# Turning a row of attention weights: by way of DRAM, or straight from place to place on chip

## The chip, the cores and the metric

The kernel runs on one core of one Trainium2 chip. A core has five engines that work side by side and wait for each other by semaphores: TensorE (PE, with its weight loads as PEld), VectorE (DVE), ScalarE (ACT), GpSimd (POOL) and SyncE (SP). Here SP does almost nothing but issue transfers; sixteen DMA engines carry them out. The metric is the time of one launch on the device in microseconds (us), median of several runs; less is better.

## The reference, cut to what matters

Two layers work on a graph of 3327 nodes with 256 features. Layer 0 makes two steps. In each, a full matrix and a sparse attention matrix are multiplied with the features:

```
A = _top_p_attention(Xa, W1, W2, W3)   # softmax(q k^T), smallest entries dropped, 0.9 of the mass kept
Xf = R @ Xf                            # R = (adj + I), rows normed
Xa = A @ Xa
Z = Z + Xf @ U1[n].T + Xa @ U2[n].T
```

Layer 1 is a graph attention over the neighbours in adj with 4 heads. All is float32.

The change touches A @ Xa. TensorE sums over partitions, so a tile of A has to lie with its columns (the nodes summed over) on the partitions. The softmax and the search for the cut need it the other way: rows on the partitions. So each block of A must be turned on the way.

## The kernel before, in words

**Tiles.** The 3327 nodes are padded to 26 tiles of 128. One "row" is a tile of 128 nodes of A, an array `e` of 128 partitions by 3328 floats (13,312 bytes per partition). There are 26 rows in each of the two steps, 52 in all. Every row goes through the same stages:

1. `logits` and `exps`: TensorE makes 128 x 3327 logits, ScalarE their exponentials into `e`.
2. `count`, `step`, `window`, `sort`, `choose`: ScalarE, GpSimd and VectorE find the cut.
3. `drop`: VectorE sets what is under the cut to zero, in three parts (columns 0 to 1023, 1024 to 2047, the rest).
4. The turn. VectorE's transpose turns 32 x 32 blocks in place, each within its own 32 partitions (`turn_blocks`, L1082). After that every block is right inside but stands in the wrong group of 32 partitions. In the kernel before, `put_blocks` (L1086) writes a part of the row to an array `blocks` in DRAM, and four `get_blocks` (L1091) read it back, one for each group of 32 partitions, each with 256-byte pieces. Per row that is three puts and twelve gets.
5. `attend_blocks` (L1098): 26 matrix products, one for each tile of columns, into one PSUM accumulator `acca`; then `attended` (L1102) scales the sum.
6. `finish1` or `finish2`: projections for the next step, or the layer norm for layer 1.

Beside it runs R @ Xf: `Full` loads each row tile of adj, turned already by the host, in seven transfers of four column tiles into four buffers `at` (L1117) and multiplies (L1123) into `accf`. These products don't wait for a row of A, so they fill TensorE while rows are being searched.

After both steps comes layer 1 (`attend_neighbours`): masks from adj (L1678, L1688, L1689), exponents on VectorE (L1700), products on TensorE (L1716, L1730).

**Order.** No engine chooses at run time. `Plan` takes every piece of work with an engine, a length, a rank, what it needs, which buffers it takes and gives, and a lag until others see its result, runs through time with these charges, and writes out one fixed order for each engine. On the chip each engine then follows its list and stops at the first piece whose data isn't there. For SP this means that a transfer at the head of the list holds back all transfers behind it, such as loads of `at`. The charges that matter here: a put 0.5 us with a lag of 8.0, a get 0.6 with 5.5, a load of `at` 0.4 with 4.0.

**Semaphores of transfers.** The transfers use eight semaphores in turn; one that takes up a semaphore waits for the transfer eight places before it.

**Buffers.** Five arrays hold rows `e` (four from `epool`, the fifth, `qq`, from `wpool`); a row keeps its array from its logits to its last attend. Small things are held in pools: `et` (three of 2 KB per partition, used for the statistics' copies, the masks of layer 1 and some loads), `f` (three), `at` (four).

Of the kernel before, what the change touches and what calls it, by code (L numbers as in the profile page):

```python
# [10 lines left out]
F32 = mybir.dt.float32  # L11
BF16 = mybir.dt.bfloat16
# [3 lines left out]
ALU = mybir.AluOpType  # L16
AX = mybir.AxisListType
PSUM = bass.MemoryType.PSUM

P = 128  # L20
N = 3327
NT = 26
NP = NT * P
D = 256
DA = 64
# [21 lines left out]
PIECES = 16  # L47
PART = 1024
PIECE_AT = [PART * (k // 5) + 205 * (k % 5) for k in range(PIECES)] + [N]
QUANTILE = (6.4004942, -10.1694914, 9.3637353, -4.4723851)  # L50

REACH = 40.0

BUFS = dict(kk=2, e=4, sc=6, f=3, xa=2, xt=2, kq=3, ystage=2, base=1, mv=4, cum=2)

# [531 lines left out]
def fast(  # L587
# [58 lines left out]
    with ExitStack() as l0:  # L646
        wpool = l0.enter_context(tc.tile_pool(name="wpool", bufs=1))
        small = l0.enter_context(tc.tile_pool(name="small", bufs=2))
        epool = l0.enter_context(tc.tile_pool(name="epool", bufs=4))
        scr = l0.enter_context(tc.tile_pool(name="scr", bufs=1))  # L650
        apool = l0.enter_context(tc.tile_pool(name="apool", bufs=4))
        etpool = l0.enter_context(tc.tile_pool(name="etpool", bufs=3))
        ps_l = l0.enter_context(tc.tile_pool(name="ps_l", bufs=2, space=PSUM))
# [8 lines left out]

        kt = wpool.tile([P, 3 * 512 + P], F32, name="kt")
        kks = [wpool.tile([P, P + 2], F32, name=f"kk{k}") for k in range(2)]
        for kk in kks:
# [3 lines left out]
        rsum = wpool.tile([P, NT], F32, name="rsum")  # L669
        blocks = spill.tile([NT // 2, P, 2 * P], F32, name="blocks")  # L670

        gks = [wpool.tile([P, 2 * DA + 1], F32, name=f"gk{n}") for n in range(STEPS)]
        for gk in gks:
            GP.memset(gk, 0.0)
            GP.tensor_copy(gk[:DA, DA + 1 :], ident[:DA, :DA])

        stat = wpool.tile([P, 2, NT], F32, name="stat")
        sig, zadd, cn, cs = (wpool.tile([P, NT], F32, name=n) for n in ("sig", "zadd", "cn", "cs"))
# [19 lines left out]
        def weights():  # L698
            held = {}
            w1 = etpool.tile([P, 4, P], F32, name="et")  # L700
            w1 = w1[:, 0, :].rearrange("p (c o) -> p c o", c=2)
# [48 lines left out]
        def layer1_loads():  # L750

            late = wpool.tile([P, 2 * D + 2 * (H * FH + 2 * H)], F32, name="late")
            g_all, b_all = late[:, :D], late[:, D : 2 * D]
            wa = late[:, 2 * D :].rearrange("p (c o) -> p c o", c=2)
            a_all = etpool.tile([P, H, 2 * FH], F32, name="et")
            nc.sync.dma_start(g_all, ln_g.partition_broadcast(P))
            nc.sync.dma_start(b_all, ln_b.partition_broadcast(P))
            nc.sync.dma_start(a_all, gat_a.partition_broadcast(P))
            nc.sync.dma_start(wa[:, :, : H * FH], gat_w.rearrange("(c p) o -> p c o", p=P))
            return g_all, b_all, wa, a_all  # L760

        def layer1_scores(wa, a_all):

            prod = etpool.tile([P, 2, H, FH], F32, name="et")
            for k in range(2):
                for a in range(2):
                    V.tensor_mul(
                        prod[:, 0],
                        wa[:, k, : H * FH].rearrange("p (h f) -> p h f", h=H),
                        a_all[:, :, a * FH : (a + 1) * FH],  # L770
                    )
                    lo = H * FH + a * H
                    V.tensor_reduce(wa[:, k, lo : lo + H], prod[:, 0], AX.X, ALU.add)

# [34 lines left out]
        def stats(n, lo, hi, rank, needs, scaled):  # L809
# [13 lines left out]
            def copy(held, m):  # L823
                qg = etpool.tile([P, 4, P], F32, name="et").rearrange("p a b -> p (a b)")
                held["qg"] = qg[:, : 3 * (2 * DA + 1)].rearrange("p (a b) -> p a b", a=3)
                S.copy(held["qg"][:, :m, :], held["ps"][:, :m, :])
# [10 lines left out]
            for t0 in range(lo, hi, 2):  # L837
                held, m = {}, min(2, hi - t0)
                a = plan.put("PE", 0.25 * m, rank, product, held, t0, m, needs=[needs, scaled], take=["px"])
                a = plan.put("ACT", 0.45, rank, copy, held, m, needs=[a], take=["et"], give=["px"])  # L840
                ends.append(plan.put("DVE", 0.35 * m + 0.2, rank, square, held, t0, m, needs=[a], give=["et"]))

# [21 lines left out]

        plan = Plan(dict(rows=1, mvs=3, pl=2, px=2, acca=1, accf=1, et=3, at=4, y=1, e2=2, ec=1, mask=2, e5=1, qg=2, **BUFS))
        own_e = [[("e", "e5")[i % 5 == 2 - n] for i in range(NT)] for n in range(STEPS)]
# [3 lines left out]
        class Row:  # L870
# [7 lines left out]
            def __init__(self, n, i):  # L878
                self.n, self.i, self.pl, self.pt, self.et = n, i, {}, {}, {}

# [195 lines left out]

            def part(self, g):
                return self.e[:, g * PART : (g + 1) * PART if g < 2 else NP]

            def turn_blocks(self, g):  # L1080
                part = self.part(g).rearrange("p (g s t) -> p g t s", s=P, t=2)
                V.transpose(part, part)  # L1082

            def put_blocks(self, g):
                src = self.part(g).rearrange("p (g w) -> p g w", w=2 * P)
                nc.sync.dma_start(blocks[4 * g : 4 * g + src.shape[1]].rearrange("g p w -> p g w"), src)  # L1086

            def get_blocks(self, g, o):
                to = self.part(g)[o * P // 4 : (o + 1) * P // 4].rearrange("p (c w) -> p c w", w=P // 2)
                src = blocks[4 * g : 4 * g + to.shape[1] // 4, :, o * P // 2 : (o + 1) * P // 2]  # L1090
                nc.sync.dma_start(to, src.rearrange("g (b s) w -> s (g b) w", b=4))  # L1091

            def attend_blocks(self, js):
                for j in js:
                    if j == 0:
                        self.acc = ps_a.tile([P, D], F32, name="acca")
                    lhs = self.e[:, j // 2 * 256 : (j // 2 + 1) * 256].rearrange("p (q t) -> p t q", t=2)[:, j % 2, :]
                    T.matmul(self.acc, lhs, rhs[self.n][:, j, :], start=(j == 0), stop=(j == NT - 1))  # L1098
# [419 lines left out]
        def attention(row, rank, total, drops, right):  # L1518
            a = None
            come = []  # L1520
            for g in range(3):
                b = plan.put(
                    "DVE", 1.17 if g < 2 else 1.44, rank - 1.001, row.turn_blocks, g, needs=[drops[g]]
                )
                b = plan.put("SP", 0.5, rank - 1.0, row.put_blocks, g, needs=[b], lag=8.0)
                b = plan.put("", 0.0, -90.0, lambda: None, needs=[b], lag=0.0)
                come.append(
                    [plan.put("SP", 0.6, rank - 1.0, row.get_blocks, g, o, needs=[b], lag=5.5) for o in range(4)]
                )
            for j in range(0, NT - 2, 4):  # L1530
                js = range(j, j + 4 if j < 20 else NT)
                a = plan.put(
                    "PE", 0.432 * len(js), rank, row.attend_blocks, js, needs=[come[j // 8], a, right],
                    take=["acca"] * (j == 0), give=[own_e[row.n][row.i]] * (j == 20),
                )
            return plan.put("ACT", 0.4, rank - 2.7, row.attended, needs=[a, total], take=["xa"], give=["acca", "sc"])
# [26 lines left out]
        def attend_neighbours(rows, ends, done, fulls):  # L1563
# [80 lines left out]
            for b in range(4):  # L1644
# [14 lines left out]
                for j in range(NT):  # L1659
# [21 lines left out]

                    def mask(held=held, off=off):
                        m = etpool.tile([P, 4, P], F32, name="et").rearrange("p a b -> p (a b)").bitcast(BF16)
                        m = held["mask"] = m[:, :W]
                        A, B = (held.pop(g).rearrange("p i q -> p (i q)") for g in range(2))
                        A, B = A[:, off:], B[:, : W + off - 4 * P]
                        for to, src in ((m[:, : 4 * P - off], A), (m[:, 4 * P - off :], B)):
                            S.activation(src, src, AF.Relu)  # L1688
                            S.activation(to, src, AF.Sign)  # L1689
# [48 lines left out]

                    own = ["et", "mask"]
                    if b == 0 and j < 2:  # L1740
                        loads, own = plan.put("SP", 0.2, rank, load_first, needs=[opened[0]], lag=4.0), []
                        m_ = plan.put("ACT", 1.8, rank, mask_first, needs=[loads])
                    else:
# [197 lines left out]
        for n in range(STEPS):  # L1941
# [30 lines left out]
            if n == 0:  # L1972
# [21 lines left out]
                def layer1():  # L1994
# [6 lines left out]
                layer1_ready = plan.put(  # L2001
                    "DVE", 3.7, base + 5.0, lambda: layer1_scores(late["wa"], late["a"]), needs=[a], take=["et"],
                    give=["et", "et"],
                )
# [74 lines left out]
```

## Time and profile before

| what | value |
|---|---|
| runs, median (lowest to highest) | 2112.4 us (2110.24 to 2112.68) |
| profiled execution, own time | 2112.06 us |
| its span in the profile | 2110.3 us |
| granted TensorE clock | 0.992 |
| PE busy | 2033.4 us (96%) |
| DVE busy | 1693.6 us (80%) |
| ACT busy | 1297.6 us (61%) |
| POOL busy | 1028.4 us (49%) |
| transfers | 361.61 MB, 637,551 packets |
| of them under 512 bytes | 373,706 packets |

A page of the profile tells, for one execution, how long each engine worked, which groups of instructions took the time, and what ended each idle stretch of an engine. "PE acca L1098 <- DMA e<-blocks" reads: TensorE stood before an instruction of line 1098 that writes `acca`, and the last thing it had waited for was a transfer from `blocks` into `e`. Idle time of an engine that nobody waits for costs nothing. SPq is SP's queue of transfers to issue: its times are those of issuing, not of moving the data.

### The profile page before, as it was taken

Reading aid. Unit: us, or ns where it says so; the run is one execution under the profiler, and the core shown is the slowest. Engines: PE = TensorE matmul, PEld = TensorE weight load, DVE = VectorE, ACT = ScalarE, POOL = GpSimd, SP = SyncE. Lnnn points to the kernel's source line nnn. Section 1 sums busy time; section 2 is a strip of 40 time slices with the busy share of each in tenths; the row PEclk is TensorE's granted clock in tenths of the full one; section 3 lists DMA queues with packets and bytes.
Section 4 is the critical chain, followed back from the end, with each engine's and each line's share of the span. In section 5 each row is a group of like instructions: output and inputs, shape, how many; then the busy total and the mean of one; then the engine's idle time right before and its main releaser. Section 6 shows DMA issues by size and latency. Waiting matters only on the chain. (4 is left out here: it accounts for less than half of the span.)

```text
span 2110.3 us, 33982 instructions
## 1 busy us (share of the span) xinstructions
PE 2033.4 (96%) x10519; PEld 1398.5 (66%) x10519; DVE 1693.6 (80%) x3768; ACT 1297.6 (61%) x2630; POOL 1028.4 (49%) x2222
## 2 busy tenths in 40 slices
PE   8999999999999889999999999999888999999997
PEld 6477778777787777778878787777776333333332
DVE  5579899887987734788778888888787989999894
ACT  4776685577656307873777777776552447464642
POOL 4367676566665404777577767777672000000001
PEclk9999999999999999999999999999999999999999
DMA  3189889888888975999879898887899444444340
GB/s 95 52 190 212 187 199 216 187 199 190 191 207 180 216 174 161 195 211 220 171 180 200 180 215 188 197 202 175 187 231 203 120 132 138 132 136 119 117 123 27
DMA packets 637551, 361.61 MB, mean 171 GB/s; under 512 B 373706, under 2 KB 590320, under 8 KB 637360
## 3 DMA queue, kind: packets, MB, share of 16 engines
q1 hardware_dynamic: 636464, 359.13, 72.8%
q8 instruction: 86, 1.41, 0.3%
q14 instruction: 105, 0.86, 0.1%
q10 hardware_dynamic: 896, 0.21, 0.0%
HBM read 254.39 MB, written 104.58 MB: 170 GB/s over the span
## 5 line engine op out<-in xcount | busy, mean ns | idle before, releaser
L1098 PE MATMUL acca<-rhs,e 128*128 128x256 f32 x2184 | 489.6, 381 | 18.1 <-DMA e<-blocks 7.0
L956 ACT ACTIVATE junk<-e,sc 128x3327 fp8e5<-128x3327 f32 x147 | 450.8, 3066 | 54.4 <-POOL sc L993 53.0
L1098 PEld LDWEIGHTS acca<-rhs,e 128*128 128x128 f32 x2184 | 425.6, 197 | 70.3 <-issue 13.8
L1123 PE MATMUL accf<-main,at 128*128 128x257 f32 x1352 | 322.2, 387 | 13.0 <-DMA at<-in_adjt_dram 6.7
L1123 PE MATMUL accf<-c,at 128*128 128x256 f32 x1352 | 311.8, 385 | 17.4 <-DMA at<-in_adjt_dram 9.0
L1123 PEld LDWEIGHTS accf<-main,at 128*128 128x128 f32 x1352 | 252.0, 192 | 75.2 <-issue 18.3
L1123 PEld LDWEIGHTS accf<-c,at 128*128 128x128 f32 x1352 | 254.7, 192 | 69.6 <-DMA at<-in_adjt_dram 11.9
L1019 DVE MAX8 cands<-y 128x8 f32<-128x205 f32 (+1 forms) x832 | 242.7, 361 | 3.7
L1014 DVE SCALAR_TENSOR_TENSOR y<-e,sc 128x1639 f32<-128x1639 f32 x84 | 167.3, 1991 | 68.2 <-POOL sc L1004 67.1
L1879 POOL TENSOR_TENSOR qq<-qq 128x256 f32<-128x256 f32 x4 | 2.9, 728 | 432.6 <-ACT qq L1875 432.6
L1716 PE MATMUL pl<-e,main 128*64 128x416 f32 x1024 | 191.6, 517 | 0.0
L1689 ACT ACTIVATE et<-at 128x448 bf16<-128x448 f32 (+1 forms) x204 | 112.2, 550 | 127.6 <-DVE e L1700 71.7
L919 ACT ACTIVATE e<-pl 128x1024 f32<-128x1024 f32 x126 | 137.6, 1099 | 65.7 <-PE pl L904 64.1
L904 PE MATMUL pl<-kt,qg 64*128 64x512 f32 (+1 forms) x832 | 173.7, 536 | 2.8 <-ACT e L919 2.8
L1082 DVE STREAM_TRANSPOSE e<-e 128x1024 f32<-128x1024 f32 (+1 forms) x126 | 168.6, 1338 | 7.1 <-POOL sc L993 0.5
L1070 DVE SCALAR_TENSOR_TENSOR e<-e,thr 128x1024 f32<-128x1024 f32 (+1 forms) x126 | 171.0, 1357 | 1.5 <-issue 0.4
L1716 PEld LDWEIGHTS pl<-e,main 128*64 128x64 f32 x1024 | 69.3, 137 | 110.5 <-issue 95.7
L1688 ACT ACTIVATE at<-at 128x448 f32<-128x448 f32 (+1 forms) x204 | 110.6, 542 | 45.3 <-DMA at<-in_adjt_dram 44.0
L1700 DVE SCALAR_TENSOR_TENSOR e<-c,low,et 128x832 f32<-128x832 f32 x128 | 129.4, 1070 | 8.1 <-issue 6.2
L1700 DVE SCALAR_TENSOR_TENSOR e<-qq,low,et 128x832 f32<-128x832 f32 x120 | 121.8, 1077 | 10.6 <-ACT et L1689 3.8
L904 PEld LDWEIGHTS pl<-kt,qg 64*128 64x128 f32 x832 | 71.4, 186 | 88.1 <-issue 74.7
L1102 ACT ACTIVATE xa<-acca,sc 128x256 f32<-128x256 f32 x52 | 24.2, 466 | 158.3 <-PE acca L1098 158.3
(547 smaller groups left out, 3436.6 us busy)
## 6 DMA issues: line engine op xcount, KB each, us to landing
at<-in_adjt_dram SPq DMA_DIRECT2D x414, 256.0 KB
blocks<-e SPq DMA_DIRECT2D x84, 512.0 KB
e<-blocks SPq DMA_DIRECT2D x336, 128.0 KB
blocks<-e SPq DMA_DIRECT2D x42, 640.0 KB
e<-blocks SPq DMA_DIRECT2D x168, 160.0 KB
at<-in_adjt_dram SPq DMA_DIRECT2D x102, 192.0 KB
blocks<-qq SPq DMA_DIRECT2D x20, 512.0 KB
qq<-blocks SPq DMA_DIRECT2D x80, 128.0 KB
```

What stands on the lines that cost most here:

```text
L904: T.matmul(pl[:, lo : lo + m], qg[self.n, self.i // 4][half, self.i % 4, :], kt[half, 512 * k : 512 * k + m], start=True, stop=True,)
L919: S.activation(to, pl.rearrange("p (g t q) -> p g t q", g=4, t=2), AF.Exp, accum_out=sums[k])
L956: S.activation(junk[:, :N], self.e[:, :N], fn, bias=t, scale=-1.0, accum_out=dst, saturate=False)
L1014: V.scalar_tensor_tensor(self.y[:, : hi - lo], self.e[:, lo:hi], self.up, self.e[:, lo:hi], ALU.is_lt, ALU.mult, accum_out=(self.h0, self. ...
L1019: V.max(self.cands[:, a * PIECES // 2 + k, :], self.y[:, at[k] - lo : at[k + 1] - lo])
L1070: V.scalar_tensor_tensor(piece, piece, self.thr[:, at : at + 1], piece, ALU.is_gt, ALU.mult)
L1082: V.transpose(part, part)
L1098: T.matmul(self.acc, lhs, rhs[self.n][:, j, :], start=(j == 0), stop=(j == NT - 1))
L1123: T.matmul(self.acc[:, : self.w], self.at[j // JC][:, j % JC, :], self.src[:, j, : self.w], start=(j == 0), stop=(j == NT - 1),)
L1689: S.activation(to, src, AF.Sign)
L1700: V.scalar_tensor_tensor(held["e"][:, k, :], extra["both"][b % 2][:, k, :], low[:, j, k : k + 1], held["mask"], ALU.max, ALU.mult,)
L1716: T.matmul(q["acc"][a][k * FH : (k + 1) * FH, c, :C], main[:, j, h * FH : (h + 1) * FH], held["e"][:, h, c * C : (c + 1) * C], start=(j == 0),
```

## The change: what it does

**Moves.** The array `blocks` in DRAM, `put_blocks` and `get_blocks` are gone. A row is turned in two parts, columns 0 to 1791 and 1792 to 3327 (`half`, `HALF = 1792`), with two transposes per row in place of three. Then `move(h, q)` issues four transfers, each from one group of 32 partitions to another: 32 partitions x 7 pieces of 256 bytes in the first part (56 KB), x 6 in the second (48 KB). With q from 0 to 3 that is 16 transfers per part and 32 per row. The first part goes into a new buffer `et` of 7 KB per partition, of which there is one; the second goes into the place that the first has left in the row's own array. So the second part's moves need the first's to have read their source, and the first part of the next row needs the attend of columns 0 to 1791 to be over.

**Attend.** The pieces of attend are cut at tile 14: tiles 0 to 13 read `et` and give it back, 14 to 25 read the row's array.

**Places.** Two pools are allocated earlier, `qq` is allocated at the front of its pool, and an unused tile `room` is added. As laid out, measured in bytes past a multiple of 256: `e` 224 before and 0 after, `qq` 160 and 0, `at` 64 and 0, `qg` 192 and 0, `rows` 224 and 0, `et` 64 and 0; `ystage` and `base` 96 and 128. `rhs`, `c` and `kt` are at 0 in both. `kq` and `f` stay at other places.

**Smaller buffers.** `f` has two buffers in place of three; the statistics' copies use `f` and no longer `et`; masks of layer 1 alternate between two places in the array `junk`, which the first two masks used already; `a_all` and `prod` of layer 1 share one `et`.

**Order.** In the planner's list for SP a row's 32 moves mostly stand in one run, with the loads of `at` in runs of three to seven between rows; before, single loads stood between the groups of four gets. SP has 2557 transfers to issue in place of 1673.

```diff
-            def put_blocks(self, g):
-                src = self.part(g).rearrange("p (g w) -> p g w", w=2 * P)
-                nc.sync.dma_start(blocks[4 * g : 4 * g + src.shape[1]].rearrange("g p w -> p g w"), src)
-
-            def get_blocks(self, g, o):
-                to = self.part(g)[o * P // 4 : (o + 1) * P // 4].rearrange("p (c w) -> p c w", w=P // 2)
-                src = blocks[4 * g : 4 * g + to.shape[1] // 4, :, o * P // 2 : (o + 1) * P // 2]
-                nc.sync.dma_start(to, src.rearrange("g (b s) w -> s (g b) w", b=4))
+            def half(self, h):
+                return self.e[:, h * HALF : HALF if h == 0 else NP]
+
+            def turn_blocks(self, h):
+                half = self.half(h).rearrange("p (g s t) -> p g t s", s=P, t=2)
+                V.transpose(half, half)
+
+            def move(self, h, q):
+                if (h, q) == (0, 0):
+                    self.first = etpool.tile([P, HALF], F32, name="et")
+                src = self.half(h).rearrange("p (g o w) -> p g o w", o=4, w=P // 2)
+                to = (self.e if h else self.first)[:, : src.shape[1] * 2 * P]
+                to = to.rearrange("p (g b w) -> p g b w", b=4, w=P // 2)
+                for k in range(4):
+                    o, b = (k, q) if h == 0 else (q, k)
+                    nc.sync.dma_start(to[o * 32 : (o + 1) * 32, :, b, :], src[b * 32 : (b + 1) * 32, :, o, :])
...
-            for g in range(3):
...
-                b = plan.put("SP", 0.5, rank - 1.0, row.put_blocks, g, needs=[b], lag=8.0)
...
-                    [plan.put("SP", 0.6, rank - 1.0, row.get_blocks, g, o, needs=[b], lag=5.5) for o in range(4)]
...
+            for h in range(2):
+                b = plan.put("DVE", 1.98 if h == 0 else 1.72, rank - 1.001, row.turn_blocks, h, needs=[drops[h + 1]])
+                a, own = b, []
+                for q in range(4):
+                    a = plan.put(
+                        "SP", 1.55, rank - 1.0, row.move, h, q, needs=[b, a, come[0][q] if h else None], take=["et"] * (h + q == 0), lag=3.5
+                    )
+                    own.append(a)
+                come.append(own)
+            a = None
+            for j in (0, 4, 8, 12, 14, 18, 22):
+                js = range(j, 14 if j == 12 else min(j + 4, NT))
                 a = plan.put(
-                    "PE", 0.432 * len(js), rank, row.attend_blocks, js, needs=[come[j // 8], a, right],
-                    take=["acca"] * (j == 0), give=[own_e[row.n][row.i]] * (j == 20),
+                    "PE", 0.432 * len(js), rank, row.attend_blocks, js, needs=[come[j >= 14], a, right],
+                    take=["acca"] * (j == 0), give=["et"] * (j == 12) + [own_e[row.n][row.i]] * (j == 22),
                 )
```

## The prediction

> **What bounds the kernel now.** First the busy times by stretch, to see which engine is full and where. The columns are the stretch in us, its length, then busy us (instructions) of PE, PEld, DVE, ACT and POOL, the granted clock, the DMA engines' busy share and GB/s.
>
> ```profile
> 0.00:90.00 90.00, 84.09 (x363) 50.18 (x365) 41.10 (x157) 50.98 (x129) 37.11 (x123) 1.00 0.20 57
> 90.00:1640.00 1550.00, 1490.17 (x6820) 1183.02 (x6818) 1232.01 (x3125) 1002.59 (x1911) 982.22 (x2089) 0.99 0.87 195
> 1640.00:2110.00 470.00, 459.17 (x3342) 165.32 (x3338) 420.49 (x488) 244.05 (x592) 9.07 (x10) 0.99 0.40 115
> ...
> 250.00:400.00 150.00, 149.36 (x683) 117.30 (x683) 133.63 (x335) 101.83 (x193) 105.23 (x210) 1.00 0.88 197
> ...
> 700.00:800.00 100.00, 87.16 (x373) 70.41 (x373) 47.10 (x141) 17.94 (x28) 20.02 (x42) 0.95 0.78 175
> ...
> 1500.00:1550.00 50.00, 42.58 (x189) 35.81 (x188) 34.94 (x77) 30.29 (x55) 39.26 (x82) 0.96 0.84 193
> ```
>
> The 52 rows lie between 90 and 1640 us. There TensorE is the bound: 1490.2 of 1550 us busy, 149.4 of 150 in the steady stretch from 250 on. It stands still for 59.8 us in all, mostly where a step ends (12.8 us in 700:800, 7.4 in 1500:1550). That is the most the change can win unless it makes matrix work itself shorter, which it doesn't touch. The DMA engines are at 0.87.
>
> Next, who TensorE waits for there (total us, times, longest), and who SP waits for over the whole span:
>
> ```profile
> PE accf L1123 <- DMA at<-in_adjt_dram: 15.7, 8, 3.8
> PE acca L1098 <- DMA e<-blocks: 7.0, 11, 1.5
> ...
> PE acca L1098 <- DMA qq<-blocks: 1.2, 3, 0.4
> ```
>
> ```profile
> SPq L1117 <- PE accf L1123: 236.1, 172, 6.7
> SPq L1086 <- DVE e L1082: 216.8, 76, 10.0
> ```
>
> Only 23.9 us of TensorE's idle time is put down to transfers: 15.7 to `at`, 8.2 to the row's own blocks. SP often stands at a put whose transpose isn't done (216.8 us, and 61.0 for `qq`), and every load behind it stands too.
>
> Last, what one issue costs on SP (ns min/median/max):
>
> ```profile
> L1091 SPq DMA_DIRECT2D e<-blocks x504: 303/507/3138, 110.1 to 1616.4; - x168
> L1086 SPq DMA_DIRECT2D blocks<-e x126: 359/377/1047, 103.3 to 1604.0; - x126
> ```
>
> ```profile
> L1234 SPq DMA_DIRECT2D qg<-kq x8: 461/496/551, 15.1 to 26.2; - x8
> ```
>
> The last line is the kernel's only transfer from one on-chip place to another, between the two halves of 64 partitions.
>
> [...] 256-byte packets into `e` at 224 have a floor of 18 ns and a mean of 28.1, 1 KB packets have 46 ns both in `rhs` (aligned) and in the puts. [...] The 512-byte packets of qg<-kq took 32.6 ns, loads from DRAM of that size 28.2 in the last stage, so the trace doesn't support a gain per packet. [...] 256-byte packets take as long as those of 512[...]
>
> **The change part by part.**
>
> *Bytes.* A put writes 128 partitions x 13 pieces of 1 KB, so 1664 packets per row and 86,528 in all, at 52.2 ns (mean of that size in the packet records) over 16 engines: 282 us of 1550, or 0.18 of the DMA engines' time. All of it goes. The 6656 packets of 256 bytes per row stay, now read on chip. I keep 28 ns for them; the ends are the floor of 18 (another 0.14 off the share) and 45 (0.24 more, 512-byte packets' slow group at 40 to 48 ns being the nearest sign). So the share falls from 0.87 to 0.69 (0.55 to 0.93).
>
> *Loads of adj.* From issue to the last semaphore update a load of `at` took 4.2 us (median) in 90:1640, and 3.0 us after 1640, where the share is 0.40. With 0.69 I take the lower value, since no longer up to eight gets of 128 KB are queued ahead: 1.2 us less in each of the 8 waits, 9.6 us. Ends: 0 (the wait was SP's, not the transfer's) and the whole 15.7.
>
> *SP.* Off per row: 12 x 0.507 + 3 x 0.377 = 7.2 us. On: 32 moves. Their price isn't in the trace. The planner charges 1.55 per four, 0.39 each; gets take 0.43 into partitions 0 to 31 and 0.49 elsewhere; qg<-kq 0.50. Some 0.037 lies between two issues in a run. I take 0.44 with the gap (ends 0.33 and 0.54): 14.1 us. That is 6.9 us more. With seven loads at 0.376 and some five others at 0.45 a row takes 19.0 us of SP, of the 29.8 that it lasts (1550 / 52). SP isn't the bound. But in a run of 32 no load of `at` gets through. Four full `at` buffers hold 4 x 4 products of 0.437 us, 7.0 us, logits another 5 and the attend of tiles 0 to 13 6.1: 18.1 us of cover against 14.1 + 3.0 for the first load behind the run. It just fits, so I cost the run at nothing; if it is dearer, the rest shows as a wait (below).
>
> *Latency of a row.* Counted from the start of `drop` (1.27, 1.25, 1.51 us) and with transposes of 1.25, 1.25 and 1.51 us: before, the last put goes out at 8.1 us, lands 3.8 later, four gets at 0.66 follow, and the last lands 5.8 after its issue: 19.7. After: transposes of 2.03 and 1.77 (1.02 ns per element by the two measured sizes), first move at 4.6, first part there at 4.6 + 16 x 0.44 + 2.4 = 14.0, second at 4.6 + 14.1 + 2.4 = 21.1, where 2.4 is the landing of qg<-kq. So the row is 1.4 us later, not earlier. In the steady stretch other work covers that; the 8.2 us of waits for blocks stay as they are. At the two ends of a step I charge it once each: +2.8, less 3 x 0.2 us of transposes: +2.2.
>
> *The turn.* Per row 2.03 + 1.77 = 3.80 against 4.01 us on VectorE: 11 us in all, hidden, since TensorE is the bound; above counted where it isn't.
>
> *Waits.* The gets' wait for the put's landing goes (it stood on SP, with loads behind it), as does one of three stops for a transpose per row: I count -2.4, a third of the 6.7 us that TensorE waited for `at` in 700:800, where SP stood 15.6 us at puts. New is that a row's first move waits for the attend of the row before (`et` has one buffer): `et` is held 7.0 + 2.4 + 6.1 = 15.5 of 29.8 us, so free in time. TensorE's list has 108 more waiting instructions (568 for 460) at 51 ns, 5.5 us, ahead of which products are queued: 0.
>
> *Small buffers.* `f` with two: one sum per row and two copies of statistics per four rows, 30 us apart, 0. Masks: at most two were in work before (beyond the first two, whose places were extra); ACT makes one in 2.2 us, VectorE uses one in 4.3, so 0 in steady state and up to 3 us at the start of layer 1. Aligned loads: within the `at` term.
>
> Sum: -9.6 + 2.2 - 2.4 = -9.8. The profiled execution took 2112.06 us (span 2110.3 and 1.8 around it), 0.3 under the median, so I put the same difference on both: 2102.
>
> **The rivals.**
>
> *Hidden anyway.* The waits for `at` come from SP's order and not from the transfers' speed: in 700:800 SP stood at a put while TensorE ran dry. Then the relief of the DMA engines buys nothing, +2.2 and -2.4 cancel, 2112. For it: 0.88 share and 99.6% busy TensorE live together in 250:400.
>
> *The run of moves starves TensorE (slower).* If a move takes 0.54 us, as 0.50 of qg<-kq plus the gap says, the run lasts 17.3 us; the first load behind it lands at 20.3, against the cover of 18.1: 2.2 us short. The second part is there 8.6 us after the first, and the first's products last 6.1: 2.5 us more. It starts to decide at 0.47 per move, (18.1 - 3.0) / 32. If a third of 52 rows pay 2.2 us, that is +38: 2150 without the gains above, 2140 with them. For it: the measured price of the nearest form; against it: single logits or products of R often stand between the two parts.
>
> *It doesn't do what it says.* Moves of 32 partitions read and write one quarter of the partitions at a time; with 45 ns a packet the DMA share is 0.93, loads land no sooner, moves land late: SP's eight semaphores then hold it. +8: 2120.
>
> **How the numbers follow.** Likeliest 0.48 (own range 2078 to 2107, the lower end with 18 ns and all waits for transfers gone and half of the idle time at the steps' ends); hidden 0.15; starved 0.26 (2115 to 2165); dearer packets 0.11. The range 2076 to 2150 leaves out about 2 in 10. A difference of 0.2% (4.2 us) is about what a measurement of this kernel can tell from none. Faster: nearly all of the first case, and a little of the second, 0.49; same: 0.14; slower: 0.37.
>
> **What would show it.** Right: packets at 551,000, DMA share in the middle near 0.69, TensorE's waits for `at` at 6 us or less in the rows' stage, SP's issues of moves at 0.40 us in the median, a row's second part there 21 us after its first drop. Wrong: moves over 0.47 us with TensorE waiting for `at` or for `et<-e` once per row; a busy sum of PE that changes; a mean of 256-byte packets far from 28 ns; or a planner's order that uses the shorter hold of the rows to close the gaps at the steps' ends, which I haven't counted.

## The result and the profile after

| what | before | after |
|---|---|---|
| runs, median (lowest to highest) | 2112.54 us (2110.24 to 2113.63) | 2465.32 us (2459.69 to 2467.03) |
| profiled execution, its span | 2112.06, 2110.3 us | 2467.03, 2465.2 us |
| granted TensorE clock | 0.992 | 0.938 |
| PE busy | 2033.4 us | 2148.3 us |
| transfers | 361.61 MB, 637,551 packets | 273.12 MB, 565,174 packets |

After stands to before as 1.1667 (95% interval 1.1646 to 1.1688): slower by 353 us, far outside the predicted range.

Nearly all of it lies in the rows' stage. The first product of line 1730 (1737 after), in layer 1, starts at 1632.8 us before and at 1983.8 after: 351.0 of the 354.9 us by which the span grew. Divided as TensorE's time, the 354.9 us are 240.0 more of standing still (2465.2 - 2148.3 = 316.9, before 76.9) and 114.9 more of work. First the stretches of the profile after (columns as in the prediction: stretch, length, busy us of PE, PEld, DVE, ACT and POOL, granted clock, DMA share, GB/s).

```profile
250.00:400.00 150.00, 132.39 (x588) 101.94 (x588) 122.18 (x309) 90.82 (x183) 82.26 (x185) 0.97 0.42 114
90.00:1970.00 1880.00, 1585.37 (x6726) 1244.48 (x6724) 1206.35 (x3043) 993.78 (x1894) 937.59 (x2085) 0.92 0.40 110
```

In the stretch from 250 to 400 us, where TensorE was busy for 149.4 of 150 us with 683 products, it is now busy for 132.4 with 588. A row takes 36.2 us (1880 / 52) in place of 29.8. No engine is busy all the time, and the DMA engines' share has fallen to 0.40. Something that the busy times don't show sets the pace. The next view is who waits for whom (total us, times, longest), first TensorE, then SP:

```profile
PE acca L1105 <- DMA e<-e: 84.0, 28, 5.7
PE acca L1105 <- DMA et<-e: 69.4, 23, 8.0
PE accf L1130 <- DMA at<-in_adjt_dram: 42.5, 11, 8.1
PE acca L1105 <- DMA kqs<-kq: 29.1, 7, 5.7
PE acca L1105 <- DMA qq<-qq: 20.2, 7, 5.1
PE acca L1105 <- DMA et<-qq: 19.7, 6, 5.5
```

```profile
SPq L1124 <- PE accf L1130: 373.3, 145, 10.3
...
SPq L1096 <- DVE e L1086: 22.0, 7, 5.5
```

TensorE's wait before `attend_blocks` for moved blocks is now the largest: 84.0 + 69.4 + 20.2 + 19.7 = 193.3 us, and with `kqs<-kq` 222.4 us. No product of line 1105 reads `kqs`; its transfer goes out right behind a row's last move, so I count that line with the moves. Before, the same waits were 8.2 us. The waits for `at` rose by 26.8 us. Together that is 241 us, the 240 within the small waits. SP in its turn stands for 373.3 us at loads of `at` until TensorE gives a buffer back (236.1 before), so each of the two waits for the other. SP's number alone is no sign of a loss: the run with half as many transfers, below, has a larger one and beats the kernel before.

The price of an issue on SP says why (ns min/median/max):

```profile
L1096 SPq DMA_DIRECT2D et<-e x672: 585/607/2071, 105.9 to 1959.8; - x168
L1096 SPq DMA_DIRECT2D e<-e x672: 585/604/1862, 116.5 to 1970.2; - x168
```

A move takes 0.605 us of SP, and never less than 0.585. The gets before, of the same 32 partitions and 256-byte pieces but from DRAM, took 0.49 in the median with 16 pieces and 0.65 with 20. One row in the timeline of SP (start, length, instruction), and beside it TensorE:

```profile
602.58 10.38 SPq L1096 DMA_DIRECT2D et<-e  x16
613.06 10.86 SPq L1096 DMA_DIRECT2D e<-e  x16
...
625.60 9.13 SPq L1124 DMA_DIRECT2D at<-in_adjt_dram  x4
...
638.20 10.38 SPq L1096 DMA_DIRECT2D et<-qq  x16
```

```profile
614.55 6.29 PE L1105 MATMUL acca<-rhs,et 128*128 128x256 f32 x28 [1.73 <-DMA et<-e]
...
625.57 7.06 PE L1105 MATMUL acca<-rhs,e 128*128 128x256 f32 x24 [3.86 <-DMA kqs<-kq]
632.46 1.90 PE L1130 MATMUL accf<-main,at 128*128 128x257 f32 x8
```

The 32 moves hold SP from 602.58 to 623.92, 21.3 us or 0.67 per move with the gap. TensorE attends the first part and does four products of R (1.03 us); then its list demands the second part of the row, so it stands for 3.86 us, until the last moves have landed (625.57). It attends until 632.63, and only the products of R behind that free buffers of `at`. Four loads, 1.5 us of issuing, thus take SP 9.13 us, and the next run begins at 638.20. The round is 35.6 us: 21.3 of moves, in which no load goes out, and 14.3 in which SP mostly waits for TensorE.

The other 115 us are TensorE's own work, 105.7 of them in the attend. The median product takes what it took before, but the mean has grown. First before, then after:

```profile
L1098 PE MATMUL acca<-rhs,e 128*128 128x256 f32 x2184 | 489.6, 381 | 18.1 <-DMA e<-blocks 7.0
```

```profile
L1105 PE MATMUL acca<-rhs,et 128*128 128x256 f32 x1456 | 369.4, 416 | 110.2 <-DMA et<-e 69.4 <-DMA et<-qq 19.7 <-DMA e<-e 15.2
...
L1105 PE MATMUL acca<-rhs,e 128*128 128x256 f32 x1008 | 279.1, 440 | 110.7 <-DMA e<-e 68.8 <-DMA kqs<-kq 29.1 <-DVE thr L1066 4.1
```

The second number behind the bar is the mean of one in ns (neighbours overlap: before, 2184 of 381 ns are 832 us, and the busy time is 489.6): 381 before, 416 and 440 now, with the median at 379 in both and single ones up to 793, twice as much. The trace's clock record has 57 stretches at half clock ahead of the end, of 3.4 or 6.8 us, 300 us in all; before there were 6, with 27 us. The 406 products of line 1105 that lie wholly within such a stretch take 634 ns in the median, the 2207 wholly outside 379. In the rows' stage such a stretch begins during or within 3 us after 41 of TensorE's 42 stops of over 3 us (up to 8.1), 15 of 26 stops between 2 and 3 us, and none of 21 between 1 and 2 us. No run here varies this alone, so that the stops bring on the half clock is my inference.

### The profile page after: what moved, and what is told of

It is laid out like the page before. It is cut to its first block, busy times and chain, and to the rows that moved or that the text cites. A ratio compares the mean times of both kernels' runs of the same rounds, so it can differ in the third digit from the quotient of the medians.

```text
span 2465.2 us, 34912 instructions
## 1 busy us (share of the span) xinstructions
PE 2148.3 (87%) x10519; PEld 1473.1 (60%) x10519; DVE 1685.4 (68%) x3705; ACT 1301.3 (53%) x2641; POOL 985.5 (40%) x2222
## 2 busy tenths in 40 slices
DMA packets 565174, 273.12 MB, mean 111 GB/s; under 512 B 387850, under 2 KB 517936, under 8 KB 564976
## 4 chain that ended last, share of the span: by engine, by line
## 5 line engine op out<-in xcount | busy, mean ns | idle before, releaser
L1105 PE MATMUL acca<-rhs,et 128*128 128x256 f32 x1456 | 369.4, 416 | 110.2 <-DMA et<-e 69.4
L1105 PEld LDWEIGHTS acca<-rhs,et 128*128 128x128 f32 x1456 | 310.3, 216 | 168.0 <-issue 107.4
L1105 PE MATMUL acca<-rhs,e 128*128 128x256 f32 x1008 | 279.1, 440 | 110.7 <-DMA e<-e 68.8
L1130 PE MATMUL accf<-c,at 128*128 128x256 f32 x1352 | 318.7, 392 | 42.6 <-DMA at<-in_adjt_dram 39.6
L1105 PEld LDWEIGHTS acca<-rhs,e 128*128 128x128 f32 x1008 | 227.4, 229 | 157.1 <-issue 75.0
L1130 PEld LDWEIGHTS accf<-c,at 128*128 128x128 f32 x1352 | 261.8, 197 | 92.4 <-DMA at<-in_adjt_dram 44.9
L1130 PEld LDWEIGHTS accf<-main,at 128*128 128x128 f32 x1352 | 254.7, 193 | 63.3 <-issue 14.1
L1696 ACT ACTIVATE junk<-at 128x448 bf16<-128x448 f32 (+1 forms) x204 | 112.5, 552 | 172.8 <-DVE e L1707 106.3
L1086 DVE STREAM_TRANSPOSE e<-e 128x1792 f32<-128x1792 f32 x84 | 160.9, 1916 | 5.0
L1137 POOL TENSOR_TENSOR at<-at,ident 128x128 f32<-128x128 f32 x52 | 25.1, 483 | 290.9 <-DMA at<-in_adjt_dram 144.4
L1707 DVE SCALAR_TENSOR_TENSOR e<-c,low,junk 128x832 f32<-128x832 f32 x128 | 129.3, 1072 | 4.9 <-issue 3.2
```

The costliest lines, as they stand in the source:

```text
L1086: V.transpose(half, half)
L1130: T.matmul(self.acc[:, : self.w], self.at[j // JC][:, j % JC, :], self.src[:, j, : self.w], start=(j == 0), stop=(j == NT - 1),)
L1707: V.scalar_tensor_tensor(held["e"][:, k, :], extra["both"][b % 2][:, k, :], low[:, j, k : k + 1], held["mask"], ALU.max, ALU.mult,)
```

## The experiments

Theory A: the number of issues on SP, at what one really costs, sets the time. The first rival, B: the planner was told 1.55 us for four moves where four take 2.65, so the order that it wrote doesn't fit the chip, and with a fitting order the moves cost little. (2.65 is four times the 0.65 to 0.67 us from one move to the next.) Others (what the transfers carry, their pieces, their landing) are spelled out in each expectation.

**The true charge.** The kernel after, with the planner told what a move takes.

```diff
-                        "SP", 1.55, rank - 1.0, row.move, h, q, ..., lag=3.5
+                        "SP", 2.65, rank - 1.0, row.move, h, q, ..., lag=2.1
```

> The changed kernel, with only the planner told what the moves cost in its profile: 2.65 us for four with a lag of 2.1, in place of 1.55 and 3.5. Theory A (SP's issuing of 32 moves, 0.67 us each from start to start, sets the pace of a row): the order changes, the 21.3 us of issuing per row stay, so the time stays within 5% of the changed kernel's 2465 us: 2350 to 2480. Theory B (a wrong charge made a bad order, and a good order hides the moves): most of the 353 us lost come back, 2120 to 2200.

Measured: 2237.18 us, 1.0595 times before (1.0560 to 1.0631). TensorE's waits in it:

```profile
PE acca L1105 <- DMA e<-e: 42.6, 17, 4.9
PE accf L1130 <- DMA at<-in_adjt_dram: 13.0, 6, 7.8
...
PE acca L1105 <- DMA et<-e: 10.6, 6, 4.1
```

Neither range was hit. The order now often lets loads of `at` through between groups of four and eight moves; 21 unbroken runs of 32 are left where there were 41. So 228 of the 353 us hang on an order made with a wrong price and lag; 125 remain with the right ones.

**Half as many transfers.** The order and buffers of after, but pieces of 512 bytes, so 16 transfers per row with the same bytes. Left out: blocks lie in wrong places, so A is not multiplied as the reference has it; the first step's projections read the input features, and the path for inputs that the fast one can't handle is closed off.

```diff
-                src = self.half(h).rearrange("p (g o w) -> p g o w", o=4, w=P // 2)
+                src = self.half(h).rearrange("p (g o w) -> p g o w", o=2, w=P)
...
-                for k in range(4):
...
+                for k in range(2):
...
```

> The changed kernel in its own order and with its own buffers, but a half of a row is moved by 8 transfers of 512-byte pieces in place of 16 of 256-byte pieces: the same bytes between the same groups of partitions, half as many issues. The blocks come to lie in wrong places, so the attention of the rows isn't the reference's; the first step's projections read the input features in place of it, and the way to the general kernel is closed. Theory A (number of issues): 16 x 0.67 = 10.7 us less on SP per row, so a row is bound by TensorE again and the time falls to 2095 to 2180 us. Theory C (the moving itself on chip, its bytes and landing): 2400 us or more. Theory D (one buffer et, two buffers f, the cut of the attend at tile 14): 2400 us or more, since all of these stay.

Measured: 2075.15 us, 0.9828 (0.9795 to 0.9861).

```profile
L1097 SPq DMA_DIRECT2D e<-e x336: 585/604/1809, 112.5 to 1576.7; - x168
```

```profile
PE accf L1131 <- DMA at<-in_adjt_dram: 9.6, 2, 6.7
```

An issue costs what it did, there are half as many, and TensorE's waits for moved blocks are down to 3.6 us (1.9 for `qq<-qq`, 1.7 for `et<-e`), in the planner's unchanged order. SP stands for 439.3 us at loads of `at` here, more than in the kernel after, and TensorE is busy for 2024 of 2076 us: here SP's standing is slack. The time came out below A's range. Two things besides the number changed. Pieces and landing did, which the next run and the last take up. And the charge of 1.55, still in place, now roughly fits what it stands for, two moves at 0.65 us: this run can't tell A from B.

**One piece.** 32 transfers again, each of one contiguous stretch per partition, so that only the form of a transfer changes (omissions as in the run before).

```diff
+                w = src.shape[1] // 4
...
+                    nc.sync.dma_start(
+                        to[o * 32 : (o + 1) * 32, b * w : (b + 1) * w], src[b * 32 : (b + 1) * 32, o * w : (o + 1) * w])
```

> The changed kernel in its own order, 32 transfers per row as before, but each moves one contiguous piece per partition (1792 or 1536 bytes) in place of 7 or 6 pieces of 256 bytes. Blocks in wrong places, the first step's projections from the input features and the general kernel closed off, as in the run with half as many. If an issue costs by its number of pieces or dimensions, the issue falls from 0.605 to 0.46 us (the two-dimensional move of qg<-kq in the kernel before had 0.46 to 0.55), a row's 32 issues to 16.5 us, and the time to 2200 to 2320. If it costs the same whatever is moved: 2440 to 2480. Theory C (bytes as small packets): below 2250 with the issue still at 0.6.

Measured: 2368.42 us, 1.1217 (1.1181 to 1.1254).

```profile
L1096 SPq DMA_DIRECT2D e<-e x672: 507/589/1782, 116.8 to 1873.1; - x168
```

One piece in place of seven leaves the issue at 0.589 us in the median, 0.018 less, and the time lies between the two ranges expected. The number and order of issues stay, and 256 of the 353 us stay with them. A run of 32 is 0.8 us shorter (20.8 for 21.6 in the median), some 40 us over 52 rows; where the rest of the 97 us that came back is from was not found.

**Places alone.** The kernel before with nothing but the aligned places: put and get by way of DRAM, all orders as before.

```diff
-        scr = l0.enter_context(tc.tile_pool(name="scr", bufs=1))
...
+        scr = l0.enter_context(tc.tile_pool(name="scr", bufs=1))
+        wpool.tile([P, NP], F32, name="qq")
+        small.tile([P, 8], F32, name="room", bufs=1)
```

> The kernel before, with its blocks by way of DRAM and its order, but e, qq, at, et and rows at multiples of 256 bytes (ystage and base at 128, as in the changed kernel). If places are what makes the 256-byte packets cheap (28.1 ns before, 15.9 after), they fall to 16 to 20 ns here too, the share of the DMA engines between 90 and 1640 us falls from 0.87 to about 0.72, loads of at land in about 3.3 us in place of 4.2, and the time falls by 5 to 20 us: 2092 to 2107. If the packets are cheap because source and destination are on chip, they stay at 28 ns and the time within 4 us of 2112.

Measured: 2071.97 us, 0.9815 (0.9791 to 0.9839). This beats both kernels, and the 2092 to 2107 expected. Its rows' stage, its waits and its gets:

```profile
90.00:1600.00 1510.00, 1482.01 (x6838) 1182.96 (x6836) 1234.58 (x3131) 1004.58 (x1914) 987.61 (x2089) 1.00 0.72 200
```

```profile
PE accf L1125 <- DMA at<-in_adjt_dram: 10.3, 9, 3.7
PE acca L1100 <- DMA e<-blocks: 3.1, 3, 1.7
```

```profile
L1093 SPq DMA_DIRECT2D e<-blocks x504: 302/488/3051, 111.7 to 1575.5; - x168
```

In the packet records 256-byte packets fall from 28.1 to 18.7 ns in the mean, and the DMA share from 0.86 to 0.72. A get of four column groups lands in 3.77 us (median) in place of 4.84, a load of `at` in 3.71 in place of 4.24. TensorE idles 31.4 us less over the span and works 11.5 us less, at a clock of 0.995. Layer 1 starts 41 us earlier. Which of the arrays matters was not tried. The kernel after has these places too, so measured from here its moves and their order cost 393 us.

**Moves out of place.** The reverse: after, with `e`, `at` and `et` 224 bytes past a multiple of 256 and `qq` 32.

```diff
+        wpool.tile([P, 8], F32, name="shift")
-        small.tile([P, 16], F32, name="room", bufs=1)
```

> The changed kernel with e, at and et put 224 bytes past a multiple of 256 (as e lay in the kernel before) and qq 32 past; order, buffers and transfers untouched. If places set the price of a 256-byte packet whatever its source, its mean rises from 15.9 to 24 to 30 ns. Theory A: the issues stay at 0.605 us and set the pace, the DMA engines have room (share 0.40, then up to 0.55), so the time stays within 1.5% of 2465: 2440 to 2500. Theory C: above 2560.

Measured: 2464.51 us, 1.1655 (1.1592 to 1.1719), the time of after. The 256-byte packets go from 15.9 to 23.7 ns, and TensorE's waits stay what they were: while the issues set the pace, this slowing of the transfers cost nothing.

**Whole rows.** 16 moves of 13 pieces per row from the row's array into `qq`; four arrays of rows in place of five. It computes everything.

```diff
-                for k in range(4):
-                    o, b = (k, q) if h == 0 else (q, k)
-                    nc.sync.dma_start(to[o * 32 : (o + 1) * 32, :, b, :], src[b * 32 : (b + 1) * 32, :, o, :])
...
+                for o in range(4):
+                    nc.sync.dma_start(to[o * 32 : (o + 1) * 32, :, q, :], src[q * 32 : (q + 1) * 32, :, o, :])
```

> A whole computation with straight moves in half as many issues: a row is moved as a whole, 16 transfers of 13 pieces of 256 bytes, from its own array into the array qq, which no longer holds rows of its own (four arrays for rows in place of five); the row's array is free once it is moved. The planner is told 2.65 us for four moves. Everything else as in the changed kernel, so the places are at multiples of 256 bytes. Theory A (number of issues): 16 x 0.67 = 10.7 us on SP per row, as many as the transfers of the kernel before took; with the cheap packets of aligned places the time is 2070 to 2130 us, the upper end if four arrays are too few. Theory C (moving on chip itself is slow): over 2200.

Measured: 2215.29 us, 1.0481 (1.0435 to 1.0527). The expectation was missed. An issue of 13 pieces costs 0.629 us, but the one array for moved rows ties them:

```profile
PE acca L1104 <- DMA qq<-e: 71.0, 22, 6.8
```

```profile
SPq L1095 <- PE acca L1104: 80.3, 31, 10.2
```

The first move waits until the row before is attended, and then TensorE waits for the moves. I gave it more slack (planner's lag 6.5 for 2.6) to see whether that was the order or the one array.

> The run with whole rows (2215 us: 16 moves per row into one array), with the lag after a move raised from 2.6 to 6.5. Theory E: the 95 us that TensorE stood before moved blocks there go largely, 2110 to 2160. Theory F (one array for moved rows: its moves, landing and attend, 10.6 + 2.3 + 11.4 us, follow each other, and more lag lengthens that chain to the length of a row): 2215 or more.

Measured: 2338.64 us, 1.1079 (1.1036 to 1.1121).

```profile
SPq L1095 <- PE acca L1104: 408.1, 48, 15.1
```

More slack made it slower, as expected if it is the array: moves, landing and attend of one row follow each other. SP now stands for 408.1 us at a row's first move with loads of `at` behind it. TensorE's waits for `at` are 175.6 us.

**A quarter of the moves by ScalarE's queue.** The true charge, with the moves of q = 3 issued by ScalarE.

```diff
-                    nc.sync.dma_start(to[...], src[...])
+                    (nc.sync if q < 3 else nc.scalar).dma_start(to[...], src[...])
...
```

> The changed kernel, planner told 2.65 us for four moves and a lag of 2.1 as in the run with the true charge (2237 us), and the last quarter of each half's moves, 8 of 32 per row, issued by ScalarE's queue in place of SP's. Theory A: SP has 5.3 us less per row, a row's moves are issued in 16 us in place of 21.3; ScalarE has 5.2 us more on some 19 per row and is not full. The time falls from 2237 to between 2110 and 2190. Theory B2 (what is left after the true charge is the latency of a row or the one buffer et, not SP's issuing): 2225 to 2250; it could rise above that if ScalarE, standing at a move whose data isn't there, holds its own work back.

Measured: 2350.18 us, 1.1114 (1.1037 to 1.1192), 113 us more than with the true charge alone. Missed:

```profile
SPq L1096 <- DMA et<-e: 121.9, 36, 6.4
```

Between the parts SP waits for moves of ScalarE to land, with loads behind it. In the round that SP begins at 617.2 us, its twelve moves of the first part are issued by 625.1; ScalarE issues its four only from 628.9 on. SP's next move overwrites nothing that those four read: for q = 0 to 2 the first part was read by SP's own moves. But the two queues share the eight semaphores. SP's next move takes up the one of ScalarE's first, which lands at 630.90, and starts at 630.96. TensorE's waits for `at` grow to 111.0 us. On ScalarE an issue costs 0.593 to 0.620 us as well. So this run says little about A. That a better split over two queues, or semaphores of its own for each, would pay was not tried.

**The true charge with slack**, lag 6.0 in place of 2.1.

> The run with the true charge (2237 us: 2.65 us for four moves, lag 2.1), with the lag after a move raised to 6.0, so that the order puts the attends and the next row's moves some 4 us later than the data comes. No work is added or taken away. Theory A (what is left after the true charge is SP's pace: 21.3 us of moves and some 5 of other issues of a row of 30): 2215 to 2270, since more slack issues nothing faster. Theory E (what is left is an order without slack: TensorE's list stands at an attend whenever a move is a little late): 2110 to 2170.

Measured: 2213.56 us, 1.0486 (1.0449 to 1.0523).

```profile
PE accf L1130 <- DMA at<-in_adjt_dram: 74.8, 34, 7.3
```

No wait for moved blocks is left among the large ones. In their place TensorE waits for loads of `at`. SP's list shows where these come from:

```profile
614.31 11.51 SPq L1096 DMA_DIRECT2D et<-e  x16
625.92 10.31 SPq L1096 DMA_DIRECT2D e<-e  x16
```

For 21.9 us no load gets through. The time lies just under A's range and far above E's. This is the best of the complete kernels with moves, and it is still 101 us above before.

**Places with other lags.** The planner's lags for put and get came from the unaligned transfers. With places alone, I gave it what was measured there (put 4.5, get 0.55 and 4.0), and in another run more slack (get 8.0).

> The kernel before with places at multiples of 256 bytes (2072 us), and the planner told the lags that its profile shows: 4.5 us in place of 8.0 for a put, 0.55 us and 4.0 in place of 0.6 and 5.5 for a get. TensorE stands still for only 28 us of the rows' stage there, so at most some 15 us are to be had: 2057 to 2080.

> The kernel before with places at multiples of 256 bytes (2072 us), with the planner's lag for a get raised from 5.5 to 8.0. TensorE stood still for 28 us of the rows' stage there, 3 of them before the row's blocks. Slack can only take these 3 to 10 us; more rows wait longer for their buffers: 2060 to 2085.

Measured: 2114.1 us, 1.0004 (0.9991 to 1.0016), and 2077.5, 0.9838 (0.9810 to 0.9866). With the measured lags TensorE waits 20.4 us in 22 places for `e<-blocks`, where with the old ones it waited 3.1. The expectation of a gain was wrong: lags that fit the median leave nothing for the transfers above it. (With `qq<-blocks`, these waits are 21 of the 29 us that TensorE stands longer.) The old, too long lags are worth 42 us, and longer ones nothing more.

**Idle issues.** The run with half as many, and after each move one transfer of 32 partitions by 4 bytes that nothing reads (omissions as there).

```diff
...
+                    at = 8 * h + 2 * q + k
+                    nc.sync.dma_start(room[o * 32 : (o + 1) * 32, at : at + 1], ident[b * 32 : (b + 1) * 32, at : at + 1])
```

> The run with half as many transfers, and after each of its 16 moves of a row one further transfer of 32 partitions by 4 bytes from one small array into another that nothing reads: 32 issues per row again, the bytes and the moves' own landing as in the run with half as many. What that run leaves out is left out here too (blocks lie in wrong places, the first step's projections read the input features, the general kernel is closed off). Theory A (the number of issues on SyncE sets the time, 0.6 us each): the small ones cost 0.59 to 0.65 us each, a row's run is about 20 us again, and the kernel takes 2300 to 2480 us with TensorE waiting for moved blocks and for at. Theory C (what a row's transfers carry, their pieces or their landing, sets it): the small ones carry nothing worth telling, 2070 to 2120 us. If their issue is much cheaper than 0.6 us, the time lies between and the price of an issue goes by what it carries.

Measured: 2451.44 us, 1.1622 (1.1546 to 1.1698).

```profile
L1099 SPq DMA_DIRECT2D room<-ident x832: 532/602/2193, 107.8 to 1962.6; - x167
```

```profile
PE acca L1108 <- DMA e<-e: 84.9, 24, 5.3
PE acca L1108 <- DMA et<-e: 52.0, 19, 9.2
PE accf L1133 <- DMA at<-in_adjt_dram: 44.6, 13, 8.8
```

Moving 128 bytes costs SP 0.602 us, as moving 56 KB does. With 32 issues per row back, the time of after and its waits are back, 376 us above the run with half as many, though the real moves carry what they carried there. A stands: in this order the number of issues makes the loss, not bytes, pieces or landing. B is right about the size: the order decides how many of those us are hidden. With the two orders that the planner wrote for the true price 101 to 125 us remain. Whether some other order would hide these too was not tried, so that they are due to the number alone is argued, not shown.

## Why the prediction was wrong

The forecast was 2102 us with 49 in 100 for faster. It failed at one term, the price of a move in *SP*, and at what hung on it.

*SP*: "I take 0.44 with the gap (ends 0.33 and 0.54)". Measured: 0.605 and 0.06 of gap, 0.67, above the upper end. I had drawn the ends from transfers that begin or end in DRAM, and from one of 64 partitions (0.50). Even the reading of those was short: "gets take 0.43 into partitions 0 to 31 and 0.49 elsewhere" holds for most gets of 16 pieces, but 289 of the 624 gets took over 0.54, and their mean is 0.695 us. Why some take so long is open, but the trace of before did hold dearer issues than my upper end. The run takes 21.3 us, not 14.1. "It just fits, so I cost the run at nothing": with the measured 3.07 us of landing, 21.3 + 3.1 stands against the cover of 18.1, 6.3 us short.

On 52 rows that would be 326 us, close to the 351 by which layer 1 begins later, but the closeness is partly luck. Only 41 runs of 32 are unbroken; 115 us of the loss are slower products, which this sum doesn't know; and TensorE's waits are mostly for moved blocks (222.4 us), not for the first load behind the run (42.5). Once broken up by the true charge, the runs gave 228 us back.

*The rival "the run of moves starves TensorE"* had the mechanism and the place right. Its second sum is the one that the round shows: the second part comes 16 x 0.67 = 10.7 us after the first, whose products last 6.3, so 4.4 short, less 1.0 of R; measured 3.86. It was too small three times over: in the price (0.54), in the rows that pay (a third; the profile has 71 stops at moved blocks or `kqs` in 52 rows), and in the slower products, which add 115 us to TensorE's work. Its point of 0.47 us, from which the price decides, was not tested: no run has moves of a price near it. The range should have reached to this case with a dearer move, since nothing in the trace of before bounded its price from above.

That "SP isn't the bound" was true as a sum: 21.3 + 7 x 0.376 + 5 x 0.45 = 26.2 us per row, under 29.8. The sum doesn't count what stands in SP's order behind a run, or the time that SP stands for TensorE. The charge of 1.55 stood in the diff, and I used it as a sign of the price without asking what an order made with a wrong one would do.

*Bytes*: "I keep 28 ns for them". Measured 15.9 ns, below the lower end of 18. The share is 0.40, where the longer stage also thins it: 0.40 of 36.2 us is 0.49 of 29.8, against 0.69 forecast. So the relief was larger than forecast, and didn't help. Packets were forecast at 551,000; 14,144 more are 4-byte ones, 16 for each of the 884 further transfers, and without them it is 551,030.

*Aligned places*, "within the `at` term", were the part worth having: 1.85% by themselves. For the packets into aligned arrays I kept 28 ns, though the records of before had 18 ns as floor and 28.1 as mean for packets into an array at 224; aligned, 18.7 is the mean. Why the place makes this difference is not shown.

*Loads of adj*: 3.0 us of landing forecast, 3.07 measured, as said; the gain drowned, since SP issued them late. *Latency of a row*: a row's last moves were to be there 16.5 us after its first was issued (14.1 + 2.4). It is 22.7, by the same price; the landing itself, 1.97 us, is shorter than the 2.4 taken. *The turn*: 1.92 us for the mean transpose, as costed. *Waits*: SP's stops for a transpose did fall, from 216.8 to 22.0 us at `e`, and bought nothing, because the moves held SP instead. `et` is held for 18.3 us of a round of 35.6 (15.5 of 29.8 forecast), so its one buffer is not the bound in this round. *Small buffers*: 0, as costed; layer 1's stage takes 3.9 us more at most. *Hidden anyway* fits neither kernel: with places alone, relief of the transfers does shorten the stage, and in the kernel after the issues lengthen it. *It doesn't do what it says* forecast a loss too, of 8 us, but for dearer packets; these became cheaper.

## What to carry to other kernels

Count transfers as instructions of the queue that issues them, and price the form you are going to use by a run of it. A quarter fewer bytes with half as many issues again on SP (2557 for 1673) lost 353 us here; moving arrays to multiples of 256 bytes, at no cost, won 40 in the kernel before. Where an order is written ahead, give the planner the true length of an instruction, but a lag above the median: 2.65 for 1.55, with its lag, was worth 228 us, and cutting lags to what was measured cost 42. When two engines' lists wait for each other in turn, no busy time shows the bound (TensorE's 87% was the highest in the kernel after): read both timelines side by side over one round.

## What the runs showed of the hardware

Issuing a transfer from one on-chip place to another with 32 partitions costs SP 0.59 to 0.63 us, for 128 bytes as for 56 KB, for one piece (0.589) as for 7 (0.607) or 13 (0.629). From DRAM to 32 partitions it is 0.49 (median) with 16 pieces of 256 bytes and 0.65 with 20, and a load of 128 partitions takes 0.38. A move lands 1.97 to 2.02 us (median) after its issue begins, so the 0.605 us of issuing are three tenths of that. Landings overlap, since the next move's issue begins after 0.65 to 0.67 us; issues on one queue follow each other (16 took 10.38 us), and 1664 of them at 0.67 us are 1.1 ms of SP.

A piece of 256 bytes takes 18.7 ns from DRAM into an aligned array and 28.1 into one 224 or 160 bytes past a multiple of 256; from place to place on chip 15.9 and 23.7. Pieces of 512 bytes hardly show it: 28.2 to 28.8 ns in the same four kernels, most of them layer 1's loads of `at`. On chip and aligned, small pieces were nearly as fast per byte as large ones: 256 bytes in 15.9 ns, 512 in 31.2 (half as many transfers), 1792 in 104.0 (one piece), which is 16 to 17 bytes per ns each.
